# A bias load moved behind four gathers, an index matmul one k step later, and two filler counts changed at the start of a float32 FFN kernel

## The chip, the core and the metric

The kernel runs on one core of a Trainium2 chip. The metric is the device time of one execution in microseconds (us); lower is better. A core has engines that run side by side, each through its own instructions in order: TensorE (PE, with its weight loads PEld), VectorE (DVE), ScalarE (ACT), GpSimd (POOL) and SyncE (SP), which here only starts DMAs. POOL starts DMAs as well, by a software queue (q0 in the profile); SP's and ACT's go through hardware queues (q1, q10). All of them are carried out by the same 16 DMA engines.

## The reference

All arrays are float32. `x` has 64 batches of 64 channels by 1024 columns.

```python
W = weights[condition]                       # one of 16 matrices, 64 x 64, for each batch
h = einsum('bct,bcd->bdt', x, W)             # conditional projection
logits = h @ gate_w.T + expert_bias          # 4 experts
one_hot = one_hot(argmax(logits), 4)
base_out = einsum('bth,oh->bto', h, W_up)    # 1024 x 1024
z = einsum('nh,erh->ner', h, lora_A)         # rank 8 for each expert
delta = einsum('neh,ne->nh', einsum('ner,ehr->neh', z, lora_B), one_hot)
out = x + base_out + delta
```

## The kernel before

**Tiles.** Two batches make a row block of 128 rows (32 row blocks); two row blocks make a group g (16 groups). The kernel multiplies `x` by one wide matrix `w` of 1060 columns first (gate, LoRA A and W_up side by side) and applies the 64 x 64 condition matrices to that product, `u`, afterwards. For a group the left operand is a 2 x 2 arrangement of blocks (A11 and A12 are the two halves of row block 0's 1024 contraction steps, A21 and A22 those of row block 1), the right one is `w` in B11, B21 (left 530 columns) and B12, B22. Later groups use a Strassen-like scheme with seven products; groups 0 and 1 take eight plain ones (`eight`) while the sums of `w` are being built.

**Precision.** Each operand is split in a high part (a cast on ACT: `ah`, `hB`, `uh`) and a low part (the difference, on DVE: `al`, `lB`, `ul`). A product is three matmuls: high with high, high with low, low with high. A block product has four k steps, each with 264 and 266 columns.

**The first step.** In group 0 the first two steps each work on two row blocks at once: step 0 on A11 and A21 with B11, step 1 on A12 and A22 with B21. One k step of such a pair is 12 matmuls. Steps 2 to 5 are single products.

**Order.** The engines keep the order in which the program calls them (the class `InOrder`; every instruction that it records shows the line of its helper, L43, in the profile, so the profile's rows are told apart by tile names). `run` goes through the steps; `product` issues a k step's matmuls and then calls the hooks registered for it with `at(step, k, function, ...)`. k = -1 is ahead of the step.

**Around the change.** `keep_warm(n)` issues n matmuls of a 128 x 128 tile of zeros on PE, whose result is not used; `WARM` of them open the program. `make_idx` is one small matmul (`batch` by `condf`) that spreads the 2 conditions of each row block over its 128 rows, and an addition on DVE that makes `idx`, the row numbers in the table of condition matrices. `load_cond(i)` starts POOL's gather of row block i's 128 rows by `idx` into `wsel`. `split_cond(i)` makes from `wsel` the block-diagonal matrices `bd` (two casts on ACT, two differences on DVE for each row block). `u_of` casts a finished product to `uh` and `ul`. `apply(i, 0)` multiplies a first piece of u by `bd` with three matmuls into the tile `o`. `gate(i)` reads its first columns: logits plus `bias_sb`, the maximum, the choice of expert, `z`; `turn(i)` transposes z on PE. `bias_sb` is the expert bias, broadcast to 128 rows by one DMA of POOL. On ACT, `split_cond` of row blocks 0 and 1 comes ahead of the cast of B22's first block and of `u_of(0)`; on DVE, `gate(0)` comes behind B22's second block.

On DVE and ACT the blocks split during step 0 come in the order B11 k = 1, A11, B11 k = 2, A21, B11 k = 3, A12, B21 k = 0, A22, and then the rest of B21. One DMA loads A12 and A22 together; SP issues it behind B11 and ahead of B21.

Of the kernel before, what the change touches and what calls it, by code (L numbers as in the profile page):

```python
# [15 lines left out]
P = 128  # L16
# [3 lines left out]
E, R = 4, 8  # L20
# [6 lines left out]

COLS = ((0, 356), (356, 352), (708, 352))
LAST = ((0, 356), (356, NB - 356), (NB, 258), (NB + 258, NB - 258))
WARM = 28  # L30
GATE = (("lg", E), ("mx", 1), ("sc", E), ("m2", 1), ("zm", ER))
HALVES = (slice(0, 64), slice(64, 128))

# [13 lines left out]
def kernel(  # L47
# [28 lines left out]
    tensor, vector, scalar, pool, sync = (  # L76
        InOrder(tc, e) for e in (nc.tensor, nc.vector, nc.scalar, nc.gpsimd, nc.sync)
    )
# [176 lines left out]
    def u_of(i, hf, c):  # L255
        u_split(i, half(hf), body(c))
# [128 lines left out]
    def keep_warm(n):  # L385
        for _ in range(n):
            tensor.matmul(wps[:, :P], warm, warm, start=True, stop=True)

    keep_warm(WARM)

# [79 lines left out]
    for e in range(E):  # L470
        pool.memset(rank[:, e : e + 1], float(E - e))
    bias_sb = cpool.tile([P, E], F32, name="bias_sb")
    pool.dma_start(bias_sb, bias.to_broadcast([P, E]))
    b3 = cpool.tile([3 * ER, H], F32R, name="b3")

    PARTS = slice(0, COLS[0][1] - G), slice(COLS[0][1] - G, H)
# [14 lines left out]
    def run(g, order, hooks, c):  # L491
        for s, step in enumerate(order):
            step = step if isinstance(step, list) else [step]
            for n, _, _, first in step:
                if first:
                    c[n] = chain()
            for kk, fn, *args in hooks[s]:
                if kk < 0:
                    fn(*args)
            product(g, [(c[n], l, r, first) for n, l, r, first in step], hooks[s])  # L500
# [4 lines left out]
    def eight(g):  # L505
        a, b = 2 * g, 2 * g + 1
        h = [[] for _ in range(6 if g == 0 else 8)]

        def at(s, k, fn, *args):
            h[s].append((k, fn, *args))  # L510

        def each(s, k, fn, q, ks, *args):
            for i in ks:
                at(s, k, fn, q, i, *args)

        one, two = (0, 1), (2, 3)
        if g == 0:
            each(0, -1, load_b, "B12", range(KH))
            at(0, 0, keep_warm, 5)
            for n in pieces:  # L520
                at(0, 0, split_b, "B11", 1, n)
            at(0, 0, make_idx)
            for i in range(4):
                at(0, 0, load_cond, i)
            at(0, 0, split_a, g, "A11", STEPS[2])
            each(0, 0, split_b, "B11", (2,))
            at(0, 0, split_a, g, "A21", STEPS[2])
            each(0, 0, split_b, "B11", (3,))
            at(0, 0, split_a, g, "A12")
            each(0, 0, split_b, "B21", (0,))  # L530
            at(0, 1, split_a, g, "A22")
            each(0, 2, split_b, "B21", (1, 2))
            each(0, 3, split_b, "B21", (3,))
            each(1, -1, load_b, "B22", range(KH))
            at(1, 0, load_b3)
            for i in (2, 3):
                at(1, 0, load_half, i, 0)
            each(1, 0, split_b, "B12", (0,))
            each(1, 1, split_b, "B12", (1,))
            each(1, 2, split_b, "B12", two)  # L540
            at(1, 2, split_cond, a)
            at(1, 3, split_cond, b)
            each(1, 3, split_b, "B22", (0,))
            at(2, -1, lambda: u_of(a, 0, c["1"]))
            at(2, 0, load_two, 0)
            at(2, 0, load_two, 1)
            each(2, 0, split_b, "B22", (1,))
            at(2, 2, apply, a, 0)
            at(2, 2, gate, a)
            at(2, 2, lambda: u_of(b, 0, c["2"]))  # L550
            at(2, 3, split_b3, PARTS[0])
            at(3, 1, turn, a)
            for i in (2, 3):
                at(3, 0, load_half, i, 1)
            each(3, 1, split_b, "B22", two)
            at(3, 2, split_a, g + 1, "A11")
            at(3, 3, delta, a, 0)
            at(3, 3, evict, a, 0)
            at(3, 3, split_b3, PARTS[1])
            at(4, 1, apply, b, 0)  # L560
            at(4, 1, gate, b)
            at(4, 2, split_a, g + 1, "A21")
            at(5, -1, lambda: u_of(a, 1, c["3"]))
            at(5, 0, turn, b)
            at(5, 0, sum_t1, one)
            at(5, 0, load_two, 2)
            at(5, 0, load_two, 3)
            at(5, 2, delta, b, 0)
            at(5, 2, evict, b, 0)
            at(5, 2, end_t1, one)  # L570
            at(5, 3, split_a, g + 1, "A12")
            at(5, 3, finish, a, 1)
            order = (
                [("1", "A11", "B11", True), ("2", "A21", "B11", True)],
                [("1", "A12", "B21", False), ("2", "A22", "B21", False)],
                ("3", "A11", "B12", True),
                ("1", "A21", "B12", True),
                ("3", "A12", "B22", False),
                ("1", "A22", "B22", False),
            )  # L580
        else:
            p = a - 1
            at(0, -1, lambda: u_of(p, 1, cs[g - 1]["1"]))
            at(0, 1, finish, p - 1, 2)
            at(0, 1, split_a, g, "A22")
            at(0, 2, make_t1, two)
            at(0, 3, finish, p, 1)
            at(1, 0, finish, p, 2)
            at(1, 1, load_cond, a + 2)
            at(1, 1, load_cond, b + 2)  # L590
            for i in (b + 2, a + 2):
                at(1, 1, load_half, i, 0)
                at(2, 1, load_half, i, 1)
            at(2, 1, make_t2, one)
            at(3, -1, lambda: u_of(a, 1, c["1"]))
            at(3, 2, make_t2, two)
            at(4, -1, lambda: u_of(b, 1, c["2"]))
            at(4, 1, sums, g + 1, "S1")
            at(4, 2, split_cond, a)
            at(4, 2, split_cond, b)  # L600
            at(5, 0, sums, g + 1, "S2")
            at(5, 1, split_a, g + 1, "A11")
            at(5, 2, sums, g + 1, "S3")
            at(6, 0, split_a, g + 1, "S2")
            at(7, -1, lambda: u_of(a, 0, c["3"]))
            at(7, 0, sums, g + 1, "S4")
            order = (
                ("1", "A11", "B12", True),
                ("2", "A21", "B12", True),
                ("1", "A12", "B22", False),  # L610
                ("2", "A22", "B22", False),
                ("3", "A11", "B11", True),
                ("1", "A21", "B11", True),
                ("3", "A12", "B21", False),
                ("1", "A22", "B21", False),
            )
        run(g, order, h, c)
        cs[g] = dict(c)
# [166 lines left out]
    for g in range(2):  # L785
        eight(g)
# [46 lines left out]
```

## Time and profile before

| | |
|---|---|
| three runs | 415.14, 415.32 and 416.02 us, median 415.32 |
| the profiled execution | 415.6 us; its span, from the first instruction to the last, 413.8 us |
| PE, busy share of the span | 99% |
| DVE, ACT, POOL | 69%, 45%, 18% |
| granted TensorE clock | 0.999 |
| DMA over the span | 60.99 MB, mean 147 GB/s; 266 and 314 GB/s in the first two of 40 slices |

A row of the timeline gives start and duration in us, engine, line, operation, the tiles written and read, shape and count; in brackets the idle time of the engine ahead of it and what ended it. Rows of equal instructions are merged ("x4"), so a row's duration runs from the first start to the last end. "xx" is the tile that holds both row blocks of group 0, first half or second half. Busy shares are averages over the whole span; the change touches only its first 12 us, where the DMA engines are full.

### The profile page before, as it was taken

The page shows a single profiled execution, that of the slowest core. Times are in us where ns is not written, and L with a number is a line of the kernel's source. Part 1 is how long each engine was busy: PE and PEld are TensorE (multiplying, and loading weights), DVE is VectorE, ACT ScalarE, POOL GpSimd, SP SyncE. Part 2 cuts the span into 40 slices and gives each one's busy share as a digit, 9 for nine tenths or more (in the row PEclk, how much of TensorE's full clock was granted, in tenths as well). Part 3 has the DMA queues.
Part 4 walks back from the last instruction along what each step waited for, and adds up shares of the span by engine and source line. Part 5 has one row for each costly group of instructions (what it writes and reads, how often), then busy time and mean ns, then how long its engine had stood idle before and what let it go on. Part 6 is the DMA issues. An engine that isn't in the chain of part 4 may idle for free.

```text
span 413.8 us, 8162 instructions
## 1 busy us (share of the span) xinstructions
PE 409.4 (99%) x3193; PEld 407.9 (99%) x3193; DVE 286.2 (69%) x648; ACT 185.1 (45%) x419; POOL 74.9 (18%) x92
## 2 busy tenths in 40 slices
PE   9999999999999999999999999999999999999996
PEld 8999999999999999999999999999999999999996
DVE  5887786866767666676676767666676676766766
ACT  5846744453534445333353534445333343533531
POOL 5205412020020201102020020201102020020000
PEclk9999999999999999999999999999999999999999
DMA  8989974543656435465452556434465442555345
GB/s 266 314 288 229 242 175 87 148 121 98 174 133 169 98 89 144 128 177 125 111 124 95 171 135 174 104 84 139 126 179 135 107 122 93 170 140 149 52 101 178
DMA packets 25830, 60.99 MB, mean 147 GB/s; under 512 B 3328, under 2 KB 5344, under 8 KB 25792
## 3 DMA queue, kind: packets, MB, share of 16 engines
q1 hardware_dynamic: 18544, 41.00, 27.9%
q0 software_dynamic: 6704, 19.21, 27.1%
q8 instruction: 25, 0.41, 0.4%
q10 hardware_dynamic: 544, 0.26, 0.2%
q14 instruction: 13, 0.11, 0.1%
HBM read 43.68 MB, written 16.78 MB: 146 GB/s over the span
## 4 chain that ended last, share of the span: by engine, by line
PE 99%; DVE 0%; issue 0%
PE c L43 82%; PE o L43 17%; DVE y L43 0%; DVE warm L43 0%; DVE one L43 0%
## 5 line engine op out<-in xcount | busy, mean ns | idle before, releaser
L43 PE MATMUL c<-hT,ah 128*128 128x264 f32 x480 | 139.7, 291 | 0.0
L43 PE MATMUL c<-lT,ah 128*128 128x264 f32 x480 | 137.3, 286 | 0.0
L43 PE MATMUL c<-hT,al 128*128 128x264 f32 x480 | 137.1, 286 | 0.0
L43 PE MATMUL c<-hB,ah 128*128 128x264 f32 (+1 forms) x424 | 121.8, 289 | 0.0
L43 PE MATMUL c<-hB,al 128*128 128x264 f32 (+1 forms) x424 | 121.2, 287 | 0.0
L43 PE MATMUL c<-lB,ah 128*128 128x264 f32 (+1 forms) x424 | 119.1, 287 | 0.0
L43 PEld LDWEIGHTS c<-lT,ah 128*128 128x128 f32 x480 | 91.0, 190 | 0.0
L43 PEld LDWEIGHTS c<-hT,ah 128*128 128x128 f32 x480 | 90.9, 189 | 0.0
L43 PEld LDWEIGHTS c<-hT,al 128*128 128x128 f32 x480 | 90.7, 189 | 0.0
L43 POOL DMA_DIRECT2D y<-in_x_dram x31 | 29.7, 957 | 289.6 <-ACT y L43 284.5
L43 PEld LDWEIGHTS c<-hB,ah 128*128 128x128 f32 x424 | 80.8, 190 | 0.3 <-issue 0.3
L43 PEld LDWEIGHTS c<-hB,al 128*128 128x128 f32 x424 | 80.7, 190 | 0.2 <-issue 0.2
L43 PEld LDWEIGHTS c<-lB,ah 128*128 128x128 f32 x424 | 79.6, 190 | 0.1
L43 ACT COPY y<-o 128x352 f32<-128x352 f32 (+1 forms) x91 | 40.1, 443 | 58.2 <-PE o L43 55.1
L43 ACT CAST uh<-usum 128x530 fp32r<-128x530 f32 (+4 forms) x44 | 27.1, 616 | 69.7 <-DVE usum L43 69.7
L43 DVE TENSOR_TENSOR al<-S,ah 128x512 fp32r<-128x512 f32 x56 | 38.5, 688 | 24.1 <-ACT ah L43 24.1
L43 DVE TENSOR_TENSOR al<-xh,ah 128x512 fp32r<-128x512 f32 x46 | 31.7, 690 | 29.9 <-ACT ah L43 29.9
L43 PE MATMUL o<-uh,bd 128*128 128x356 f32 (+2 forms) x186 | 44.8, 322 | 0.0
L43 DVE TENSOR_TENSOR ul<-usum,uh 128x530 fp32r<-128x530 f32 (+4 forms) x44 | 30.1, 683 | 18.7 <-ACT uh L43 18.6
L43 ACT CAST zt<-o 96x128 fp32r<-96x128 f32 x31 | 8.1, 262 | 76.4 <-PE o L43 76.4
L43 POOL DMA_INDIRECT wsel<-in_cw_dram,idx x32 | 34.2, 1070 | 11.9 <-issue 5.2
L43 ACT CAST ah<-S 128x512 fp32r<-128x512 f32 x56 | 34.9, 623 | 1.8 <-DVE S L43 1.4
(88 smaller groups left out, 472.2 us busy)
## 6 DMA issues: line engine op xcount, KB each, us to landing
xh<-in_xt_dram SPq DMA_DIRECT2D x60, 256.0 KB
y<-in_x_dram POOLq DMA_DIRECT2D x30, 512.0 KB, 5.6
out_dram<-y SPq DMA_DIRECT2D x30, 512.0 KB
wraw<-in_w_dram SPq DMA_DIRECT2D x23, 265.0 KB
T<-in_w_dram POOLq DMA_DIRECT2D x8, 265.0 KB, 7.8
xx<-in_xt_dram SPq DMA_DIRECT2D x1, 512.0 KB
wsel<-in_cw_dram,idx POOLq DMA_INDIRECT x32, 5.0
y<-in_x_dram SPq DMA_DIRECT2D x1, 512.0 KB
```

The costliest lines, as they stand in the source:

```text
L43: return lambda *a, **k: self.tc.keep_in_program_order(fn(*a, **k))
```

## The change

The opening fillers become 30 instead of 28, and those behind the first k step 2 instead of 5. The index matmul, the addition on DVE and the four gathers are called behind k = 1 of step 0 instead of k = 0, and so behind the splits that k = 0's hooks issue. The load of the bias is issued behind the four gathers on POOL instead of ahead of them. SP's order is the same. On DVE `idx` now follows the split of B21's block k = 0.

```diff
-WARM = 28
+WARM = 30
...
     bias_sb = cpool.tile([P, E], F32, name="bias_sb")
-    pool.dma_start(bias_sb, bias.to_broadcast([P, E]))
     b3 = cpool.tile([3 * ER, H], F32R, name="b3")
...
-            at(0, 0, keep_warm, 5)
+            at(0, 0, keep_warm, 2)
             for n in pieces:
                 at(0, 0, split_b, "B11", 1, n)
-            at(0, 0, make_idx)
-            for i in range(4):
-                at(0, 0, load_cond, i)
             at(0, 0, split_a, g, "A11", STEPS[2])
             each(0, 0, split_b, "B11", (2,))
             at(0, 0, split_a, g, "A21", STEPS[2])
             each(0, 0, split_b, "B11", (3,))
             at(0, 0, split_a, g, "A12")
             each(0, 0, split_b, "B21", (0,))
+            at(0, 1, make_idx)
+            for i in range(4):
+                at(0, 1, load_cond, i)
+            at(0, 1, lambda: pool.dma_start(bias_sb, bias.to_broadcast([P, E])))
             at(0, 1, split_a, g, "A22")
             each(0, 2, split_b, "B21", (1, 2))
             each(0, 3, split_b, "B21", (3,))
```

## Prediction

> **What bounds the kernel now.** I read the page's head and its chain first, then the same chain in order of time, then the timeline of each engine over the first 25 us, because the edits lie in the first 12 us and their products are used up to 21 us.
>
> ```profile
> span 413.8 us, 8162 instructions
> PE 409.4 (99%) x3193; PEld 407.9 (99%) x3193; DVE 286.2 (69%) x648; ACT 185.1 (45%) x419; POOL 74.9 (18%) x92
> PE 99%; DVE 0%; issue 0%
> ```
>
> TensorE (PE) is the bound from end to end: 99% of the chain. A microsecond of new PE wait is therefore a microsecond on the span; a removed instruction of another engine is worth nothing unless PE waited for it. Now PE at the five places that matter (start us, duration us):
>
> ```profile
> 0.99 3.17 PE o L43 x28
> 4.18 0.56 PE L43 MATMUL c<-hB,ah 128*128 128x264 f32 x1
> 7.01 0.47 PE L43 MATMUL o<-warm 128*128 128x128 bf16 x5
> 7.41 0.18 PE L43 MATMUL o<-condf,batch 2*128 2x32 bf16 x1
> 7.53 0.39 PE L43 MATMUL c<-hB,ah 128*128 128x264 f32 x1
> 13.19 0.39 PE L43 MATMUL c<-hB,al 128*128 128x264 f32 x1
> 20.89 0.32 PE L43 MATMUL o<-ul,bd 128*128 128x356 f32 x1
> ```
>
> These are the fillers, the first product, the fillers behind it, the index matmul, k = 1, the first product with A22's low half, and the last of the three matmuls of apply(0, 0). The other engines, each from its own timeline:
>
> ```profile
> 4.20 0.62 POOL L43 DMA_DIRECT2D bias_sb<-in_bias_dram  x1
> 7.63 0.25 DVE L43 TENSOR_SCALAR idx<-o,rowf 128x32 int32<-128x32 f32 x1 [0.32 <-PE o L43]
> 8.17 1.05 POOL L43 DMA_INDIRECT wsel<-in_cw_dram,idx  x1 [2.45 <-DVE idx L43]
> 9.53 1.19 POOL L43 DMA_INDIRECT wsel<-in_cw_dram,idx  x1 [0.30 <-issue]
> 10.34 0.62 ACT L43 CAST ah<-xx 128x512 fp32r<-128x512 f32 x1 [1.36 <-DMA xx<-in_xt_dram]
> 12.45 0.69 DVE L43 TENSOR_TENSOR al<-xx,ah 128x512 fp32r<-128x512 f32 x1
> 17.27 1.04 ACT L43 CAST bd<-wsel 64x64 fp32r<-64x64 f32 x4
> 19.65 0.70 DVE L43 TENSOR_TENSOR ul<-c,uh 128x530 fp32r<-128x530 f32 x1
> DMA to landing us min/median/max: 5.2/5.6/6.3
> ```
>
> The last line is for the four gathers that read idx. See how long the gathered rows lie idle: gather 0 lands about 13.4 (8.17 + 5.2), gather 1 about 15.1 (9.53 + 5.6); ScalarE (ACT) takes the first at 17.27 and the second at 17.79 (half of 1.04 later). Last, the windows of the DMA (busy per engine, then clock, share, GB/s) and the queues over 8 to 12 us:
>
> ```profile
> 8.50:9.00 0.50, 0.50 (x6) 0.50 (x5) 0.50 (x2) 0.48 (x1) 0.50 (x1) 1.00 1.08 360
> 9.00:9.50 0.50, 0.50 (x7) 0.50 (x6) 0.50 (x2) 0.00 (x0) 0.22 (x1) 1.00 1.10 293
> q0 software_dynamic: 32, 0.00, 3.8%
> ```
>
> DMA is full there, and moves least where it is busiest. The software queue holds 3.8% of 16 engines x 4 us, 2.4 engine-us, with practically no bytes: this is the bias (2 KB), no gather's data having started. ACT meanwhile waits 1.36 us for A12/A22.
>
> [...] 28 fillers start within 3.0 us, and 264-column matmuls go from 0.22 us apart before 7 us to 0.12 after it. [...] the trace shows nothing overtaking, so a cast waiting for gathered rows holds all behind it. [...]
>
> **The change part by part.**
>
> *Front fillers, 28 to 30.* Spacing is 3.0/28 = 0.107 us. The 28 end at 0.99 + 3.00 = 3.99, the first product starts at 4.18, because its ah (DVE, 3.74 + 0.29) is ready only at 4.03. Two more end at 4.20. Cost 0 to 0.03 us; were ah early, 0.21.
>
> *Fillers behind k = 0, 5 to 2, and the index matmul away from there.* Today 7.01 to 7.53 = 0.52. Two fillers plus the switch to k = 1 are about 0.25, so k = 1 starts some 0.27 earlier (of its block, hB is ready at 6.82, and lB, in two pieces, at 6.93 and 7.32, which come later in the step). Between k = 1 and k = 2 the index matmul then costs 0.12 (7.41 to 7.53) plus 0.10 for the exposed weight load behind it. Net gain in PE's arrival: 0.05, bounds 0 to 0.15. It is worth nothing as long as PE waits at 13.19 for A22's low half (DVE, 12.45 + 0.69 = 13.14).
>
> *Index on DVE.* In DVE's queue idx moves behind A12's low half and the lB of B21 block 0, which ends at 12.53. So it ends at 12.45 + 0.25 = 12.70 instead of 7.88: 4.82 us later, though its matmul is only one k step (1.5 us) later. Behind it in the queue is A22's low half, exactly what PE waits for: up to 0.17 us more (spacing 7.63 to 7.80) if nothing else shifts.
>
> *Gathers.* All four follow idx on POOL, so each starts 4.82 later. Slack of gather 1: 17.79 - 15.1 = 2.7 at ACT. Behind its cast come the cast of B22 block 0, the cast of u (18.88), then DVE's low half of u (19.65 + 0.70 = 20.35), which PE uses at 20.89: 0.5 more, with semaphore time. So the move passes the cover by 4.82 - 2.7 - 0.5 = 1.6 us. If the later gather lands in 5.2 instead of 5.6, 1.2. SP's queue is identical; ACT's too, except for this wait.
>
> *Bias out of the way.* Without it the engine that delivers A12/A22 last may win back between 0 and about 0.85 us (1.36 us of ACT idle, 2.4 engine-us on two or three engines). That moves A12, B21, lB and idx forward together: idx at 11.85 to 12.70. It also removes the stalls around 13.19 (12.44 to 13.54 holds six matmuls, 6 x 0.123 = 0.74, so 0.36 lost), but PE then only reaches the gather wait sooner. Full relief leaves 0.4 to 0.8 of the gather wait, none 1.2 to 1.6. I take the middle, 1.0.
>
> *Bias at its new place.* It follows gather 3, at gather 0 + 4.12 + 1.08 + 0.30: with idx at 12.3, 12.6 + 5.5 = 18.1. Its old issue-to-landing isn't on the page; estimated from the gathers' 5.2 to 6.3, it lands at 23.3 to 24.4 in the worst case; a light DMA (share 0.53 at 18 to 20 us) speaks for 3 to 4 us, 21.1 to 22.1. Its reader, lg on DVE, starts at 21.25 today and at about 22.2 with the gather wait, and PE needs the gate's z only 2 us behind lg. I take 0; the bad end costs 1 to 2 us.
>
> *Sum.* Front 0, second fillers 0, gather wait +1.0, bias 0: +1.0 us. The profiled execution was 415.6 (span 413.8), inside the three runs' 415.14 to 416.02 and 0.3 above their median; the same +1.0 on the median, 415.32, gives 416.3.
>
> **The rivals.**
>
> A, the forecast: gather 1 comes last at apply(0, 0); +0.3 to +1.9 us, centre +1.0, 416.3. For it: the slack sum, all of it from rows. Against: it rests on how long a gather takes then.
>
> B, bias relief outweighs it, not slower: if A12 and B21 come 1.1 us earlier and gather 1 lands in 4.5 us, 1.1 sooner than the 5.6 of the sum, idx ends about 11.6, the excess 4.82 - 1.1 - 1.1 - 2.7 - 0.5 is below 0 (it decides from about 1.6 us won in all), and PE keeps what it gained, 0.05 + 0.36 to at most 0.6: 414.8 to 415.3. For it: the DMA dip at 9.0 to 9.5 us. Against: four gathers are issued 1.4 us apart, and the first two must both land.
>
> C, the bias too becomes late: lg waits beyond 22.7, gate and turn(0) slip, PE stops once more before step 3's second k: A plus 0.5 to 2, 417.3. It decides from a bias landing above 5 us. For it: 32 packets took 2.4 engine-us before. Against: the emptier DMA.
>
> D, clock: fewer fillers behind step 0 let PE run dry and keep the half clock longer. PE has no gap there in either order, so at most a few tenths, inside A's width; no chance of its own.
>
> **How the numbers follow.** A 0.57, B 0.26, C 0.17. The predicted time is A's centre, 416.3. About 0.2% (0.83 us) is what a measurement of this kernel can tell from no change. Of A, 0.37 lies above +0.83 and 0.20 below; all of C is above: slower 0.54. Of B 0.13 reads as no change: same 0.33. The other 0.13 of B is for relief larger than I can derive, since the runs of before alone spread over 0.88 us: faster 0.13. Range 414.7 to 417.5: B's best at one end, A plus a small part of C at the other; about 0.1 left out on each side.
>
> **What would show it.** Right: idx at 11.8 to 12.7 on DVE; the first gather at 12.1 to 13.0; ACT idle before a bd cast, released by the wsel DMA, near 17 to 19.5 us; PE waiting at apply(0, 0) for uh or ul, the third matmul at 21.5 to 22.5. A12's cast well before 10.34 would show bias relief; 12.44 to 13.54's six matmuls without gaps likewise. An idle DVE before the first lg released by bias_sb shows C. Wrong: the bd casts start without a wait, or apply's third matmul comes at or before 20.89.

## The result, and the profile after

The changed kernel takes 418.88 us (median of 7 executions, 417.26 to 420.84) against 415.58 us (median of 7 executions of the kernel before, the three above among them, 415.02 to 416.38): ratio 1.0085, 95% interval 1.0065 to 1.0106. It is slower by some 3.3 us, where +1.0 was forecast. The profiled execution was the quickest of the seven, 417.26 us (span 415.5). The head of its page:

```profile
span 415.5 us, 8160 instructions
PE 409.0 (98%) x3192; PEld 406.9 (98%) x3192; DVE 285.7 (69%) x648; ACT 184.9 (44%) x419; POOL 74.9 (18%) x92
PE 94%; DMA 2%; issue 2%; POOL 0%; DVE 0%; ACT 0%; POOLq 0%; ACTq 0%
```

PE's work is the same, but the chain that ended last has left PE for 6% of the span, a third of that in a DMA. PE's waits over the whole span (engine and tile, what it waited for, us in all, times, longest) say where:

```profile
PE o L43 <- ACT uh L43: 1.7, 1, 1.7
PE o L43 <- DVE one L43: 1.0, 1, 1.0
PE o L43 <- DVE ul L43: 0.3, 1, 0.3
```

The 1.0 is the wait for the first filler, which the kernel before has too. The other two are new and stand at one place. The timeline of PE:

```profile
4.14 0.36 PE L43 MATMUL c<-hB,ah 128*128 128x264 f32 x1
6.03 0.29 PE L43 MATMUL o<-warm 128*128 128x128 bf16 x2
6.46 0.39 PE L43 MATMUL c<-hB,ah 128*128 128x264 f32 x1
21.55 0.59 PE L43 MATMUL o<-uh,bd 128*128 128x356 f32 x2 [1.69 <-ACT uh L43]
22.42 0.43 PE L43 MATMUL o<-ul,bd 128*128 128x356 f32 x1 [0.27 <-DVE ul L43]
```

The third matmul of apply(0, 0) stands at 22.42 instead of 20.89: 1.53 us later, nearly all of the 1.7 us by which the two spans differ. The chain behind it, from the timelines of DVE, POOL and ACT:

```profile
9.46 0.62 ACT L43 CAST ah<-xx 128x512 fp32r<-128x512 f32 x1 [0.58 <-DMA xx<-in_xt_dram]
11.44 0.24 DVE L43 TENSOR_SCALAR idx<-o,rowf 128x32 int32<-128x32 f32 x1
11.97 1.28 POOL L43 DMA_INDIRECT wsel<-in_cw_dram,idx  x1 [6.20 <-DVE idx L43]
13.54 1.46 POOL L43 DMA_INDIRECT wsel<-in_cw_dram,idx  x1 [0.30 <-issue]
18.28 0.51 ACT L43 CAST bd<-wsel 64x64 fp32r<-64x64 f32 x2 [2.68 <-DMA wsel<-in_cw_dram,idx]
19.83 0.51 ACT L43 CAST bd<-wsel 64x64 fp32r<-64x64 f32 x2 [1.04 <-DMA wsel<-in_cw_dram,idx]
20.91 0.59 ACT L43 CAST uh<-c 128x530 fp32r<-128x530 f32 x1
21.66 0.70 DVE L43 TENSOR_TENSOR ul<-c,uh 128x530 fp32r<-128x530 f32 x1
22.90 0.15 DVE L43 TENSOR_TENSOR lg<-o,bias_sb 128x4 f32<-128x4 f32 x1
```

Read it from top to bottom. The bias no longer sits in the DMA engines when A12/A22 come (the software queue has no packets from 8 to 12 us, where it had 32 before): their first cast is at 9.46, not 10.34. So idx, behind it and behind B21's first block on DVE, is done at 11.68 and not 12.70. It is still 3.8 us later than before. ACT stands idle 2.68 and 1.04 us for gathered rows, with the cast of u queued behind them. lg has no wait in brackets: the bias, issued at 17.52, landed 3.6 us later. The query for the tile idx closes with the gathers' time:

```profile
  ACT bd L43: 3.7, 2
DMA to landing us min/median/max: 4.0/5.5/6.2
```

Asked for one by one, gathers 0 and 1 took the 6.2 us, gathers 2 and 3 4.8 and 4.0. Yet 1.7 us is only half of the slowdown. The granted clock (1.000 is full speed over the whole span) of the seven executions, in the order of their times, was 0.998 (417.26), 1.000 (417.39), 0.996 (418.73), 0.996 (418.88), 0.994 (419.29), 0.991 (420.63), 0.990 (420.84): what the profiled one doesn't show goes with the clock.

### The profile page after: what moved, and what is told of

Read it like the earlier page. It is cut to its first block, busy times and chain, and to the rows that moved or that the text cites. A ratio compares the mean times of both kernels' runs of the same rounds, so it can differ in the third digit from the quotient of the medians.

```text
span 415.5 us, 8160 instructions
## 1 busy us (share of the span) xinstructions
PE 409.0 (98%) x3192; PEld 406.9 (98%) x3192; DVE 285.7 (69%) x648; ACT 184.9 (44%) x419; POOL 74.9 (18%) x92
## 4 chain that ended last, share of the span: by engine, by line
PE 94%; DMA 2%; issue 2%; POOL 0%; DVE 0%; ACT 0%; POOLq 0%; ACTq 0%
PE c L43 78%; PE o L43 16%; DMA wsel<-in_cw_dram,idx 1%; DMA cond_sb<-in_cond_dram 1%; POOL wsel L43 0%; DVE ul L43 0%; ACT hB L43 0%; DVE lB L43 0%; DVE y L43 0%; ACT bd L43 0%; POOL which L43 0%; POOL condf L43 0%; POOLq L43 0%; ACTq L43 0%; POOLq L820 0%
```

## The experiments

Theory T: the gathered rows come late at apply(0, 0), which stops PE for about 1.7 us; and this stop costs clock in many executions. Rivals, with letters of their own: B, the bias at its new place comes late (the prediction called this C); F, the fewer fillers; G, a gather wait that is itself longer in the longer executions.

### One part alone, or one undone

```diff
 e1_bias_only: before, with
-    pool.dma_start(bias_sb, bias.to_broadcast([P, E]))
             for i in range(4):
                 at(0, 0, load_cond, i)
+            at(0, 0, lambda: pool.dma_start(bias_sb, bias.to_broadcast([P, E])))
 e2_index_back: e1 with WARM = 30 and keep_warm 2
 e3_index_only: before, with make_idx and load_cond at (0, 1), behind the splits of (0, 0)
 e4_fillers_only: before, with WARM = 30 and keep_warm 2
```

> The bias alone is moved behind the gathers; index matmul and fillers stay as before. Theory T (the gather of the second row block comes about 1.7 us too late at apply(0, 0), and in a part of the executions the long PE wait also costs granted clock): no late gather here, so no wait and no clock loss; the freed DMA engines bring A12/A22 at about 9.5 instead of 10.34 and take the 0.36 us of stalls at 12.4 to 13.5 away: 415.0 to 415.6, clock 0.998 to 1.0. Rival B (the late bias is what makes the changed kernel slow): lg waits, 416.5 or more.

> The changed kernel with index matmul and gathers back behind k = 0; bias behind the gathers, fillers 30 and 2. Theory T: everything above the kernel before goes away, 414.9 to 415.6, clock 0.998 to 1.0. Rival B (bias): stays above 416.5. Rival F (fewer fillers behind the first step let the clock fall in the opening): stays above 416.5 with clocks down to 0.99.

> Only index matmul and gathers are a k step later; bias in front, fillers 28 and 5. Theory T: idx at about 12.7 as DMA relief is missing, so the gather wait is 0.3 to 0.9 us longer than in the changed kernel, about 2.3 us; 418 to 421, with clocks between 0.99 and 1.0 that go with the time. Rivals B and F: not slower than 416.0.

> Only the fillers are changed (30 and 2). Theory T: 415.2 to 415.8, no clock loss. Rival F: 417 or more, clocks down to 0.99.

| kernel | median us, executions | ratio to before, 95% interval |
|---|---|---|
| before, run beside e1 to e4 | 415.74 (51) | |
| e1, bias | 414.95 (21) | 0.998, 0.9974 to 0.9987 |
| e2, bias and fillers | 414.89 (22) | 0.9982, 0.9976 to 0.9989 |
| e3, index | 419.49 (6) | 1.0088, 1.0068 to 1.0109 |
| e4, fillers | 415.82 (14) | 1.0004, 0.9994 to 1.0013 |

The four settle which part does it. The index move alone costs all that the whole change costs. The fillers are nothing. The bias move is a gain of 0.2%: B and F fall. The medians of e1 and e2 are a hair below what T gave. How the bias gains is in the windows from 9 to 10 us. A row gives the window, its length, the busy time of PE, PEld, DVE, ACT and POOL (instructions), the granted clock, the DMA's share and its GB/s. The kernel before, then e1:

```profile
9.00:10.00 1.00, 1.00 (x11) 1.00 (x10) 0.87 (x2) 0.00 (x0) 0.70 (x2) 1.00 1.01 318
```

```profile
9.00:10.00 1.00, 1.00 (x10) 1.00 (x10) 0.64 (x2) 0.62 (x2) 1.00 (x1) 1.00 1.04 399
```

Nearly the same share moves 81 GB/s more. All twelve traces agree: with the bias ahead of the gathers (before, e3, e4) the DMA moved 299 to 342 GB/s in this microsecond, with the bias behind them 388 to 405. Which load pays varies: in e4, bias ahead, A12's cast came at 9.57, nearly as early as with the bias moved, and the cast of B21's first block, at 10.85 instead of e1's 10.00, was the late one. In e1 the third matmul of apply(0, 0) starts at 19.73 instead of 20.89. Part of this lead is there before A12 comes (idx starts at 7.01 on DVE, at 7.63 in the trace of before), so the median, 0.8 us, is the better measure.

### The clock

```diff
 e9_changed_again: the changed kernel
 e5_after_filled_wait: the changed kernel with
+            at(2, 2, keep_warm, 24)
             at(2, 2, apply, a, 0)
```

> The changed kernel once more, for a second trace. Theory T: the same PE wait near 20 to 22 us within 0.4 us; where the time is over 418, the clock falls to half right behind that wait for about 3.4 us or twice that, and nowhere else. Rival G: the wait itself is longer by what the time is longer.

> The changed kernel with 24 unused filler matmuls (24 x 0.056 us = 1.3 us) ahead of apply(0, 0), where PE otherwise stands idle for 1.7 us; the wait for the gathered rows is left as it is. Theory T (the wait costs about 1.7 us in every execution, and the rest of the 3.3 us is clock lost because PE stands idle in it): the median falls to 417.0 to 417.7, the executions lie within about 1 us, and every clock is 0.998 or more. Rival G (the gather itself lands later in the slower executions, and the clock is a by-product): median stays near 418.9, times spread over 417 to 421.

e9 took 418.92 us (span 417.1), as long as the changed kernel's median. Its timeline on PE, around the wait:

```profile
21.75 0.59 PE L43 MATMUL o<-uh,bd 128*128 128x356 f32 x2 [1.76 <-ACT uh L43]
22.62 0.43 PE L43 MATMUL o<-ul,bd 128*128 128x356 f32 x1 [0.28 <-DVE ul L43]
22.89 0.34 PE L43 MATMUL c<-hT,ah 128*128 128x264 f32 x1
23.02 0.42 PE L43 MATMUL c<-lT,ah 128*128 128x264 f32 x1
23.25 0.42 PE L43 MATMUL c<-hT,al 128*128 128x264 f32 x1
23.46 0.43 PE L43 MATMUL c<-hT,ah 128*128 128x266 f32 x1
```

The wait is 0.07 us longer than in the first trace, and right behind it products that started 0.12 us apart start 0.22 apart. The windows of the same trace (third figure from the end: the granted clock):

```profile
18.00:22.00 4.00, 2.24 (x18) 2.03 (x17) 1.65 (x6) 2.41 (x7) 0.26 (x1) 1.00 0.79 231
22.00:24.00 2.00, 1.72 (x9) 1.43 (x9) 1.79 (x6) 1.09 (x3) 0.00 (x0) 0.74 1.07 382
24.00:26.00 2.00, 2.00 (x11) 2.00 (x11) 1.60 (x4) 0.00 (x0) 0.00 (x0) 0.50 0.95 318
26.00:30.00 4.00, 4.00 (x33) 4.00 (x33) 2.41 (x5) 3.08 (x7) 0.00 (x0) 0.95 0.34 128
```

Lost clock: 0.26 x 2 + 0.50 x 2 + 0.05 x 4 = 1.7 us. With the 1.73 by which apply's third matmul is late (22.62 - 20.89), that is 3.4 us, against 3.3 us between the spans of e9 and of the first trace of before. (Against the 38 executions of before that ran beside it, median 415.10, e9 is 3.8 us slower; the rest is not accounted for.) In this execution the wait is not longer, so G falls for it. e3's trace, 419.6 us, shows a fall as large: clock 0.96 from 20 to 24 us and 0.61 from 24 to 28 (0.04 x 4 + 0.39 x 4 = 1.7 us), behind a wait of 1.60 and 0.28.

The other executions of the changed kernel have no trace, but an estimate is possible. One fall, 3.41 us at half clock in e9, costs 1.7 us. The last microseconds of the span take more off the clock's mean: 0.3 us in the trace of before (clock 0.83 from 412.00 to 413.82), 1.0 in the first of the changed kernel (0.72 from 412.00 to 415.48); in e9 the mean of 0.994 leaves some 0.8 beside the fall. A clock of 0.996 or 0.994 (1.7 or 2.5 us lost of 417) then has room for one fall, 0.991 and 0.990 (3.8 and 4.2) for two. With 1.7 us taken off for each, the seven executions lie between 417.0 and 417.6: by this estimate their waits differ little, and what spreads them is the number of falls. G is not dead everywhere: one execution of e3 took 419.37 us at clock 1.000, 1.1 us more than the slower of its other two at 0.998 and above, and six of e6 (below) took 416.47 to 417.68 at 0.999 or 1.0. There the wait itself may have been longer; it was not traced.

e5 leaves the wait and fills it, so that PE is idle for only 1.0 us of it (in the trace of before, fillers start 0.107 us apart up to 3.8 us and 0.056 apart from 7.1 us on): 417.94 us (6 executions, 417.72 to 418.42), ratio to before 1.0065 (1.005 to 1.0079), every clock 0.999 or 1.0. Its PE:

```profile
19.97 1.51 PE L43 MATMUL o<-warm 128*128 128x128 bf16 x24
22.22 0.59 PE L43 MATMUL o<-uh,bd 128*128 128x356 f32 x2 [0.74 <-ACT uh L43]
23.09 0.43 PE L43 MATMUL o<-ul,bd 128*128 128x356 f32 x1 [0.28 <-DVE ul L43]
```

The clock loss is gone in all executions, as T said; the median is 0.2 us above T's upper end, since u came still later: gather 1 took 6.6 us in this trace, and the third matmul stands at 23.09, 2.2 late. That the median itself fell isn't shown: the intervals of e5 and of the changed kernel overlap.

### Where the wait comes from

```diff
 e6_index_ahead_of_a12: the changed kernel with
-            at(0, 0, split_a, g, "A12")
-            each(0, 0, split_b, "B21", (0,))
             at(0, 1, make_idx)
...
+            at(0, 1, split_a, g, "A12")
+            each(0, 1, split_b, "B21", (0,))
 e8_second_split_behind_u: the changed kernel with
-            at(1, 3, split_cond, b)
...
             at(2, -1, lambda: u_of(a, 0, c["1"]))
+            at(2, 0, split_cond, b)
 e10_two_gathers_first: the changed kernel with load_cond 2 and 3 at (5, 2), behind end_t1
 e11_back_two_gathers: e2 with the same
```

> The changed kernel with the splits of A12 and of B21's first block called behind the index matmul, so that on DVE idx comes ahead of them: still one k step later on PE, but idx at about 9.8 instead of 11.44. Theory T: gather 1 then lands 1.6 us sooner, at about 18.2 or a little before, its row block's u is ready about 20.8 against the 20.3 at which PE asks: a wait of 0 to 0.5 us, 414.9 to 415.9, no clock loss. If the k step on PE itself were what costs, it would stay above 417.

> The changed kernel with the split of the second row block's condition matrices called behind the cast of the first block's u, so that ACT and DVE don't hold that u for gather 1 (landed 19.8); gather 0 (landed 18.25) is still needed. Theory T: u is ready 1.5 us sooner, the PE wait falls from about 2 us to 0.2 to 0.7 us, 415.2 to 416.2, no clock below 0.998. Rival H (gather 0 alone is as late, order on ACT doesn't matter): above 417.

> The changed kernel with only the two gathers that the opening needs behind the index; the other two are issued at about 34 us, behind the first accumulating loads. It asks why gather 1 took 6.3 us at its new place and not the 5.2 to 5.6 of before. Bunching (gathers 2, 3 and the bias, all in flight before gather 1 has landed, hold it up): gather 1 lands in 5.2 to 5.6 us, the PE wait shrinks by 0.7 to 1.0 us, 417 to 417.8. Place (the DMA engines are busy with other loads when its packets come, or the issue itself is slower): 6.2 us again, 418 to 420 with clocks down to 0.99.

> The version with index matmul back behind k = 0 and the bias behind the gathers, with gathers 2 and 3 issued at about 34 us. There is no gather wait to win; fewer software DMAs in the full stretch may bring the loads of B21 and B12 forward, which PE doesn't wait for: 414.5 to 415.2, the same as with four gathers.

| kernel | median us, executions | range us | ratio to before, 95% interval |
|---|---|---|---|
| before, run beside e6 and e8 | 415.10 (38) | 414.69 to 416.99 | |
| e6, idx ahead of A12 on DVE | 416.48 (22) | 414.64 to 419.55 | 1.0032, 1.0015 to 1.005 |
| e8, second split behind u | 416.32 (17) | 416.03 to 416.78 | 1.0025, 1.0017 to 1.0033 |
| before, run beside e10 and e11 | 415.59 (21) | 414.69 to 416.59 | |
| e10, two gathers | 419.48 (5) | 417.43 to 420.75 | 1.009, 1.0074 to 1.0106 |
| e11, index back, two gathers | 414.74 (16) | 414.36 to 415.82 | 0.998, 0.9972 to 0.9989 |

e6 keeps the index matmul a k step later on PE and moves only DVE's part. Of its trace, one of the better executions (415.09 us), the timelines of DVE and ACT and the last line of the query for idx:

```profile
9.32 0.24 DVE L43 TENSOR_SCALAR idx<-o,rowf 128x32 int32<-128x32 f32 x1
17.65 0.51 ACT L43 CAST bd<-wsel 64x64 fp32r<-64x64 f32 x2 [1.48 <-DMA wsel<-in_cw_dram,idx]
DMA to landing us min/median/max: 5.4/6.1/7.3
```

The k step on PE is no cost of its own; most of the delay was DVE's queue. But the median is 0.6 us above T's upper end, and T's "no clock loss" missed: the six executions of e6 over 418 us have clocks of 0.993 to 0.996, the sixteen below it 0.998 to 1.0. Their waits were not traced; that the cover is now so thin that the scatter of the gather decides is the likely reason, not a shown one.

e8 confirms the order on ACT: with gather 1 taken out of u's way, 2.5 us come off the changed kernel's excess by the ratios (1.0085 - 1.0025 = 0.006 of 415), and no clock in 17 executions is below 0.998. Its ACT:

```profile
19.18 0.51 ACT L43 CAST bd<-wsel 64x64 fp32r<-64x64 f32 x2 [3.28 <-DMA wsel<-in_cw_dram,idx]
20.25 0.60 ACT L43 CAST uh<-c 128x530 fp32r<-128x530 f32 x1
20.91 0.51 ACT L43 CAST bd<-wsel 64x64 fp32r<-64x64 f32 x2
```

Gather 0 alone is late enough to leave a wait (0.7 and 0.3 us on PE), a little more than T gave: it took 6.8 us in this trace, against 6.2 in the first.

e10 shows no gain from fewer gathers in flight: gather 0 took 5.9 us and gather 1 6.2 from issue to landing, so bunching is not the reason. The gathers of one trace scatter widely (e1's four, at the old place, took 5.5 to 6.7 us), but gather 1, taken alone, goes with its place. At the old place it took 5.3 to 6.1 us (before 5.6, e1 6.1, e2 5.4, e4 5.9, e11 5.3), at the new one 6.2 to 7.0 (the changed kernel 6.2, e3 6.2, e5 6.6, e8 7.0, e9 6.3, e10 6.2). What makes it slower there stays open. e11 is, as expected, e2's equal: the versions that beat both kernels are e1, e2 and e11, about 0.8 us below the kernel before.

## Why the prediction was wrong, point by point

- *Front fillers, second fillers and index matmul on PE: about 0.* Right (e4), though PE went dry for a moment ahead of 6.46 us: in that execution products of 264 columns start 0.12 us apart already at 5.30, in the trace of before still 0.22 apart at 5.68 (the traces' clock records begin with full clock at 3.96 and at 7.03), so PE came sooner.
- *Index on DVE.* Right in kind: idx fell behind A12 and B21. Done at 11.68, 0.2 us ahead of the end of full relief (11.85).
- *Bias out of the way.* Right, and the whole of the range: A12's cast 0.88 us earlier against a bound of about 0.85. Taking half was too little. (In e4 the cast came early with the bias still ahead, so these 0.88 us can't all be put down to the bias.)
- *Bias at its new place: 0.* Right: it landed at about 21.1, 3.6 us behind its issue and ahead of lg at 22.90. The DMA was light (share 0.62 from 18 to 20 us), as argued; that this is why it took no longer was not shown.
- *Gathers, +1.0 us.* The mechanism is what was forecast, down to the cast of u held on ACT, but the term was mis-sized: 1.53 us in one trace, 1.73 in e9. It took gather 1's 5.6 us over to a place where it had not been measured, with shorter times as the only other cases (5.2, and 4.5 in rival B), though the same line shows 6.3; it took 6.2. (The 5.2 given to gather 0 belongs to gather 2; gather 0 has no landing on record in that trace, and the sum doesn't rest on it.) The sum 4.82 - 2.7 - 0.5, less the 1.0 that idx won, is 0.6; the landing of 6.2 instead of 5.6 adds 0.6, and gather 1, issued 1.57 us behind gather 0 (11.97 to 13.54) instead of 1.36, adds 0.2: 1.4 of the 1.53.
- *The step that failed: "A microsecond of new PE wait is therefore a microsecond on the span."* PE stood idle twice within 3.4 us, 1.7 and 0.3 us, and lost another 1.7 us of clock in an execution as long as the median (e9). The clock was looked at only in the opening (rival D) and given "no chance of its own". Without this loss the two fastest executions, at 0.998 and 1.000, cost 1.7 and 1.8 us over the median before, inside A and inside the range. But e5, which kept its clock, cost 2.8 us over the executions of before beside it (417.94 against 415.10), beyond A's 1.9: with a gather of 6.6 us the mis-sized gather term alone passes the range.
- *The prediction's rival B*, bias relief, was real as a gain (e1, 0.2%) but did not outweigh the gathers; *its rival C*, a late bias, did not occur.

## What to carry to other kernels

Price a moved step by where its last instruction lands in each engine's queue, not by where the first one is called: one k step on PE became nearly 4 us on DVE. Where PE is the bound, a wait of about 2 us can cost more than its length: in e9 2.0 us of it went with 1.7 us of lost clock, and five of the seven executions here had a clock of 0.996 or less. With fillers in the wait the clock was 0.999 or 1.0 in all six executions of e5, though that they gain time isn't shown. Take the latency of a gather from several traces, at the place where it will stand, and keep its cover wider than the scatter (here 4.0 to 7.3 us).

## What the runs showed of the hardware that was not expected

- The half clock came behind some waits and not behind others as long. In e9 PE was idle for 2.0 us (1.76 and 0.28), and half clock followed for 3.41 us. The window ahead and that of the half clock (the second figure is the window's length, the third PE's busy time):

```profile
19.55:22.97 3.42, 1.39 (x8) 0.89 (x7) 2.18 (x5) 2.89 (x7) 0.00 (x0) 1.00 0.87 278
22.97:26.38 3.41, 3.41 (x18) 3.41 (x17) 2.42 (x9) 0.12 (x1) 0.00 (x0) 0.50 1.00 338
```

The first trace of the changed kernel has nearly the same wait (1.69 and 0.27 us) and no fall, in the wait or behind it:

```profile
20.00:24.00 4.00, 2.17 (x14) 1.88 (x15) 3.16 (x10) 2.84 (x7) 0.00 (x0) 1.00 0.96 330
24.00:28.00 4.00, 4.00 (x34) 4.00 (x33) 3.66 (x8) 2.78 (x7) 0.00 (x0) 1.00 0.87 324
```

- So 2.0 us of idleness in e9 and 1.9 in e3 were followed by half clock; 2.0 in the first trace and 1.9 in e10 (1.6 and 0.3, clock 0.998 over the span) were not, nor the 1.0 us that e8 and e5 left (clock 1.0 in both traces). What decides among the four long waits was not shown; between 1.0 and 1.9 nothing was traced. No other execution of e8 or e5 fell either: no clock is below 0.998. The executions at 0.990 and 0.991 would need two falls, by the estimate above; none was traced with two.
- With the bias, 2 KB, ahead of the loads, the DMA moved 299 to 342 GB/s from 9 to 10 us (three traces); with it behind the gathers, 388 to 405 (nine). The move alone took 0.8 us off the median (e1), although 99% of the chain was PE.
- Gathers of 128 rows of 256 bytes took from 4.0 to 7.3 us from issue to landing in the first 20 us of these traces.
